# Layer 1's node work of a four-layer graph network, by quarters beside the output attention of layer 0

## The chip, the cores and the metric

The kernel runs on one core of a Trainium2 chip. The metric is the time of one execution on the device in microseconds (us), as the median of several runs. The core has a matrix engine (PE, with its weight loads as PEld), a vector engine (DVE), an activation engine (ACT), a general engine (POOL) and a queue engine (SP) that mostly issues DMAs. Each engine takes its instructions in a fixed order. "Unit", "quarter" and "count" below are words of this kernel; they are explained with it.

## The reference, cut to what matters

A graph of 4096 nodes with 64 features and a dense 0/1 adjacency passes through four layers, each of the form `x = x + layer(relu(layernorm(x)), adj)`.

```python
# layer 0: eight attention heads, then the output attention
Who = h @ W_out;  o1 = Who @ a_out[:64];  o2 = Who @ a_out[64:]
e_o = leaky_relu(o1[:, None] + o2[None, :], 0.2)
x = x + tanh(softmax(where(adj > 0, e_o, NEG)) @ Who)
# layer 1: hyperbolic attention over all pairs; h = relu(layernorm(x)), c = 1 / r**2
x_t = logmap0(h, c)                      # h * artanh(sqrt(c)*|h|) / (sqrt(c)*|h|)
left, right = x_t @ w_att[:64, 0], x_t @ w_att[64:, 0]
adj_att = sigmoid(left[:, None] + right[None, :] + b_att) * adj
support = einsum('ij,ijd->id', adj_att, logmap(h[:, None], h[None], c))
x = x + proj(expmap(h, support, c), c)
# layer 2: mean over neighbours, a dense layer, row norm
# layer 3: out[i] = sum over the last 100 neighbours j of 0.5**(later neighbours) * (h @ W3)[j]
```

In layer 1 each node needs a few numbers that come from its own row only: the squared norm `a`, `pc = 1 - c*a` and its inverse, the two scores, the scaled row, and two rows of 66 numbers ("sides") from which a single matmul gives the distances of all pairs.

## The kernel before

Nodes lie on 128 partitions in 32 blocks (`NB`); `x` and `h` are tiles of 128 x 32 x 64 floats. The adjacency comes transposed, and layer 0 leaves it in DRAM as eight-bit masks (`mask_d`) for the later layers. The program is written in one stream; a scheduler then orders each engine's instructions by its own estimates. Three helpers bind it: `in_order()` keeps the engines' instructions in the order of the program, and `behind(ins)` and `tc.issue_after(ins)` place the enclosed instructions after a given one.

**The output attention of layer 0** (the loop `for u in range(4)` and what is ahead of it). The setup takes the maxima of `who` (the 66 columns of `Who` and its two scores), reduces them over the partitions on POOL (`omax`), and makes from them the value parts `YB`, `YC`, the denominators' parts `YD1`, `YD2`, the mean `meano` and at last the negated values `YCn`. Then come four units of 1024 target nodes. A unit goes through eight mask tiles `mo` (`for q in range(NQ)`, 512 KB each, three buffers). For each, DVE makes the complement `nmo8`, which POOL's queue writes to `noedge_d` for layer 1; for every two of its four blocks ACT makes the sign of the score (`st`, L1198), DVE ands it with the mask (`B`, L1204, four buffers) and mostly makes the other edges (`C`, L1212), and PE multiplies (`acco`, L1961, and the denominators `ddo`, L1974 and L1980). At a unit's end the sums are copied to SBUF (`evD`, `evB`, `evC`); `finish_unit` transposes and divides them, takes tanh and adds to `x`. It runs inside the next unit, after its first mask tile; for the last unit it runs after the loop.

**The counts.** `count_odd` (L949, L950) loads 1 MB of the adjacency (`raw`, two buffers, SP's queue) and counts the entries that are neither 0 nor 1. There are 64 of them: 16 in the loop of the output attention (every second mask tile), 11 in layer 2, 37 in layer 3. A program with any odd entry is redone by a general kernel.

**Layer 1 before the pairs.** When all of `x` is there, `layernorm_relu()` makes `h` by halves (`norm_steps`). Then DVE computes over all 32 blocks at once: `a`, `pc`, the norm and its logarithms, `left` and `nrb` by `dot` (L2050, L2052). Five maxima (`way`) are reduced over the partitions (`wall`, L2102) to a flag `again`, which every engine reads before it branches (L2118, L2721). Behind the branch `pairs_fast` splits `left` in three parts, transposes them and sends them through DRAM to `MOV` (L2155, L2156); makes `XQ` (the rows scaled by `pabs`), and the sides `aug` for `XA` and `LD`, transposed on PE in 16 groups of four (L995) with one ACT copy each (L996). The tile `nm` of the mask work takes memory that `aug` held.

**Layer 1's pairs** (`scores`, `distances`, `factors`, `sums`) take about 545 us. `finish_steps` then gives the new `x` and `h` by quarters; `layers_fast` holds layers 2 and 3, with tiles `HH` and `SS` for the split rows of layer 2 and the values of layer 3, and `blk` for its counting matmuls. Layer 3 has four units of 1024 target nodes with eight masks `m3` of four blocks each; a count stands at the blocks that a condition on `j` and `u` picks.

Of the kernel before, what the change touches and what calls it, by code (L numbers as in the profile page):

```python
# [24 lines left out]
P = 128  # L25
# [805 lines left out]
def kernel(  # L831
# [200 lines left out]

    with ExitStack() as l0:
        lp = l0.enter_context(tc.tile_pool(name="l0", bufs=1))
        who = lp.tile([P, NB, D + 2], F32, name="who")
# [125 lines left out]
        def col_maxs(m, n, name):  # L1161

            full = lp.tile([P, n], F32, name=name)
            nc.gpsimd.partition_all_reduce(full, m, P, RMAX)
            return full
# [570 lines left out]

        HO2 = N // 4
        NK = HO2 // G
        OB = HO2 // P
        with ExitStack() as ob:  # L1740
# [21 lines left out]
            nc.gpsimd.memset(YD2, 0.0)  # L1762
            meano = hp.tile([P, NK, 2, D], F16, name="meano")
# [23 lines left out]
            with in_order():  # L1787
# [13 lines left out]
                m3 = col_maxs(m3, 4, "omax")  # L1801
                Mo = lp.tile([P, 1], F32, name="Mo")
# [68 lines left out]
            nc.vector.tensor_scalar(  # L1871
# [53 lines left out]
            for u in range(4):  # L1925
# [8 lines left out]
                for q in range(NQ):  # L1934
                    if q % 2 == 0:
                        count_odd(work, next(todo))
# [49 lines left out]
                    if q == 0 and pending:  # L1986
                        finish_unit(*pending)
                        pending = None
                evD = work.tile([P, G], F32, name="evD", tag="evD", bufs=1)
# [19 lines left out]
                pending = (u, evs)  # L2009
            finish_unit(*pending)  # L2010


    layernorm_relu()
    l1 = ctx.enter_context(ExitStack())
    lp = l1.enter_context(tc.tile_pool(name="l1", bufs=1))
    KA = D + 2

    def scalar_tile(name):
        return lp.tile([P, 1], F32, name=name)

    rt, rabs, sqc, cc = (scalar_tile(n) for n in ("rt", "rabs", "sqc", "cc"))
    nc.gpsimd.dma_start(rt, r_in.unsqueeze(0).to_broadcast([P, 1]))
    nc.vector.scalar_tensor_tensor(rabs, rt, -1.0, rt, ALU.mult, ALU.max)
    nc.vector.reciprocal(sqc, rabs)
    nc.vector.tensor_tensor(cc, rt, rt, ALU.mult)
    nc.vector.reciprocal(cc, cc)
    c2, m2c, p2c, cneg, lnr, bz, be, maxn, hrow = (
        scalar_tile(n) for n in ("c2", "m2c", "p2c", "cneg", "lnr", "bz", "be", "maxn", "hrow")
    )
    nc.vector.tensor_tensor(c2, cc, cc, ALU.mult)  # L2030
    nc.vector.tensor_scalar(m2c, cc, -2.0, None, ALU.mult)
    nc.vector.tensor_scalar(p2c, cc, 2.0, None, ALU.mult)
    nc.vector.tensor_scalar(cneg, cc, -1.0, None, ALU.mult)
    nc.vector.tensor_scalar(maxn, rabs, 1.0 - PROJ_EPS, None, ALU.mult)
    nc.vector.tensor_scalar(hrow, rabs, 0.5, None, ALU.mult)

    nc.scalar.activation(lnr, rabs, AF.Ln)
    nc.vector.tensor_scalar(bz, lnr, -1.0, -0.5 * SHIFT * LN2, ALU.mult, ALU.add)
    nc.vector.memset(be, 0.5 * SHIFT * LN2)
    wab = lp.tile([P, 2, D], F32, name="wab")  # L2040
    nc.gpsimd.dma_start(
        wab.rearrange("p s d -> p (s d)"),
        w_att.rearrange("k o -> (k o)").unsqueeze(0).to_broadcast([P, 2 * D]),
    )
    bt = scalar_tile("bt")
    nc.gpsimd.dma_start(bt, b_att.unsqueeze(0).to_broadcast([P, 1]))

    def dot(wide, pool, a, b, name):
        t = wide.tile([P, NB, D], F32, name=name + "_w", tag="wide")
        nc.vector.tensor_tensor(t, a, b, ALU.mult)  # L2050
        s = pool.tile([P, NB], F32, name=name)
        nc.vector.tensor_reduce(s, t, AX.X, ALU.add)  # L2052
        return s

    def norm_of(pool, sq, name):
        n = pool.tile([P, NB], F32, name=name)
        nc.vector.tensor_scalar(n, sq, MIN_NORM, None, ALU.max)
        nc.scalar.activation(n, n, AF.Sqrt)
        return n

    with tc.tile_pool(name="l1wide", bufs=2) as wide:
        a = dot(wide, lp, h, h, "a")
        pc = lp.tile([P, NB], F32, name="pc")
        nc.vector.tensor_scalar(pc, a, cneg, 1.0, ALU.mult, ALU.add)
        pm = lp.tile([P, NB], F32, name="pm")
        nc.vector.tensor_scalar(pm, pc, MIN_NORM, None, ALU.max)

        zn = norm_of(lp, a, "zn")
        nc.vector.tensor_scalar(zn, zn, sqc, None, ALU.mult)
        zr = small("zr")  # L2070
        nc.vector.reciprocal(zr, zn)
        nc.vector.tensor_scalar(zn, zn, CLIP, None, ALU.min)
        la, lb = small("la"), small("lb")
        nc.scalar.activation(la, zn, AF.Ln, bias=one_t, scale=1.0)
        nc.scalar.activation(lb, zn, AF.Ln, bias=one_t, scale=-1.0)
        nc.vector.tensor_tensor(la, la, lb, ALU.subtract)
        fac = lp.tile([P, NB], F32, name="fac")
        nc.vector.scalar_tensor_tensor(fac, la, 0.5, zr, ALU.mult, ALU.mult)
        left = dot(wide, lp, h, wab[:, 0:1, :].to_broadcast([P, NB, D]), "left")
        nrb = dot(wide, lp, h, wab[:, 1:2, :].to_broadcast([P, NB, D]), "nrb")  # L2080
        nc.vector.tensor_tensor(left, left, fac, ALU.mult)
        nc.vector.tensor_tensor(nrb, nrb, fac, ALU.mult)
        nc.vector.tensor_scalar(nrb, nrb, bt, -1.0, ALU.add, ALU.mult)
# [3 lines left out]
    pinv = lp.tile([P, NB], F32, name="pinv")  # L2087
    way = lp.tile([P, 5], F32, name="way")
# [12 lines left out]
    wall = lp.tile([P, 5], F32, name="wall")  # L2101
# [17 lines left out]

    def pairs_fast(es, VQ, VT, pabs):  # L2120

        fp = es.enter_context(tc.tile_pool(name="pf", bufs=1))
        XQ = VQ
        XA = fp.tile([KA, N], F32, name="XAf")
        LD = fp.tile([KA, N], F32, name="LDf")
        MOV = fp.tile([P, N], BF16, name="MOV")
# [5 lines left out]
        nc.vector.reciprocal(pinv, pc)  # L2132
        nc.vector.scalar_tensor_tensor(pabs, pinv, -1.0, pinv, ALU.mult, ALU.max)
        with ExitStack() as ss:
            wide = ss.enter_context(tc.tile_pool(name="pfwide", bufs=2))
            ps = ss.enter_context(tc.tile_pool(name="ps_pf", bufs=4, space=PSUM))

            parts = wide.tile([P, 3, NB], F32, name="parts")
            p16 = wide.tile([P, 3, NB], BF16, name="p16")
            tmp = wide.tile([P, NB], F32, name="ptmp")  # L2140
            lr_d = dram.tile([3, N], BF16, name="lr_d")
            nc.gpsimd.memset(MOV, 0.0)
            nc.gpsimd.memset(one3, 0.0)
            nc.gpsimd.memset(one3[0:3, :], 1.0)
            nc.vector.tensor_copy(tmp, left)
            for c in range(3):
                nc.vector.tensor_copy(p16[:, c], tmp)
                if c < 2:
                    nc.vector.tensor_tensor(tmp, tmp, p16[:, c], ALU.subtract)
            nc.vector.tensor_copy(parts, p16)  # L2150
# [570 lines left out]
    with tc.If(general == 0):  # L2721
        with ExitStack() as es:
# [12 lines left out]
            with ExitStack() as pe:  # L2735
                pairs_fast(pe, VQ, VT, pabs)
# [74 lines left out]
```

## Time and profile before

| what | value |
| --- | --- |
| timed runs | 2208.22, 2210.75, 2210.93 us; median 2210.75 |
| the profiled execution | 2203.01 us, span 2201.3 us, granted TensorE clock 0.93 |
| busy over the span | PE 87%, DVE 80%, ACT 73%, POOL 4% |
| output attention, setup | from about 931 us to `YCn` at 990 us |
| output attention, copies `evD` of the four units | 1034.0, 1082.4, 1128.6, 1172.9 us |
| first score matmul of layer 1 | 1236.3 us |
| last pairs, layer 2, layer 3 | to about 1780, 2028, 2195 us |

The profile is of one execution, 7.7 us under the median of the timed runs. Times in it are counted from the start of the span. In the table of windows each row gives the stretch, its length, the busy time of each engine with its number of instructions, the granted clock of PE, the mean share of the 16 DMA engines and what they moved. In a timeline each row is a start, a duration, engine, line, operation, tiles written and read, and in brackets how long the engine sat idle before it and on whom it waited. Lines are those of the kernel before unless it is said otherwise.

### The profile page before, as it was taken

Reading aid. Unit: us, or ns where it says so; the run is one execution under the profiler, and the core shown is the slowest. Engines: PE = TensorE matmul, PEld = TensorE weight load, DVE = VectorE, ACT = ScalarE, POOL = GpSimd, SP = SyncE. Lnnn points to the kernel's source line nnn. Section 1 sums busy time; section 2 is a strip of 40 time slices with the busy share of each in tenths; the row PEclk is TensorE's granted clock in tenths of the full one; section 3 lists DMA queues with packets and bytes.
Section 4 is the critical chain, followed back from the end, with each engine's and each line's share of the span. In section 5 each row is a group of like instructions: output and inputs, shape, how many; then the busy total and the mean of one; then the engine's idle time right before and its main releaser. Section 6 shows DMA issues by size and latency. Waiting matters only on the chain.

```text
span 2201.3 us, 43889 instructions
## 1 busy us (share of the span) xinstructions
PE 1916.3 (87%) x19276; PEld 865.8 (39%) x19276; DVE 1763.7 (80%) x2239; ACT 1608.9 (73%) x1379; POOL 85.5 (4%) x124
## 2 busy tenths in 40 slices
PE   4989989999999999939994679999999996889887
PEld 3444444444444444423442323333333332444222
DVE  6689989997898899978767688998989888744654
ACT  3678879997798799846773669888888873137655
POOL 1000100000000000000110000000000000000000
PEclk8999999999999999959996789999999997979989
DMA  8945554353111111078551101101110105722995
GB/s 110 185 97 93 101 84 112 126 188 121 45 45 45 45 50 50 11 259 306 177 183 43 35 15 34 34 25 29 34 35 24 34 19 199 289 104 97 315 329 216
DMA packets 117007, 239.00 MB, mean 109 GB/s; under 512 B 11059, under 2 KB 84003, under 8 KB 102051
## 3 DMA queue, kind: packets, MB, share of 16 engines
q1 hardware_dynamic: 101990, 192.92, 25.4%
q0 software_dynamic: 14816, 43.18, 11.2%
q8 instruction: 153, 2.51, 0.5%
q14 instruction: 48, 0.39, 0.1%
HBM read 245.34 MB, written 49.46 MB: 134 GB/s over the span
## 4 chain that ended last, share of the span: by engine, by line
PE 33%; DVE 16%; ACT 6%; DMA 5%; issue 4%; POOL 0%; DVEq 0%; SPq 0%; POOLq 0%; ACTq 0%
PE accj L2270 6%; PE acco L1961 4%; DMA raw<-in_adj_dram 4%; PE pu L2237 3%; PE pl L2206 2%; DVE raw L950 2%; PE pf L2308 2%; DVE at L2259 2%; PE pl L2209 2%; PE accC L1534 2%; PE nacc L2603 1%; ACT st L1198 1%; DVE at L2264 1%; PE accB L1534 1%; ACT sg L2193 1%
## 5 line engine op out<-in xcount | busy, mean ns | idle before, releaser
L1198 ACT ACTIVATE st<-srow,nt 128x2048 int8<-128x2048 f32 x352 | 682.7, 1994 | 77.2 <-DVE B L1204 76.4
L1204 DVE TENSOR_TENSOR B<-st,mres 128x1024 int32<-128x1024 int32 x256 | 311.9, 1221 | 68.1 <-PE accC L1534 44.9
L1534 PE MATMUL accB<-B,ybh 128*32 128x512 fp8e4 x3072 | 338.7, 384 | 14.4 <-DVE B L1204 14.4
L1534 PE MATMUL accD<-B,ybh 128*32 128x512 fp8e4 x2048 | 301.3, 387 | 23.6 <-DVE h L1650 23.6
L1534 PEld LDWEIGHTS <-ybh 128*32 128x32 bf16 (+1 forms) x6656 | 196.5, 98 | 238.4 <-issue 76.1
L1534 PE MATMUL accC<-mres,ych 128*32 128x512 fp8e4 x2272 | 268.1, 381 | 0.0
L1534 PE MATMUL accC<-B,ycn 128*32 128x512 fp8e4 x2272 | 267.9, 380 | 0.0
L1534 PE MATMUL accL<-B,ybh 128*32 128x512 fp8e4 x1536 | 220.0, 389 | 4.8 <-DVE h L1654 4.7
L2270 PE MATMUL accj<-sg,VQ 128*64 128x512 f32 (+1 forms) x512 | 199.5, 620 | 17.9 <-DVE sg L2311 7.0
L1534 PEld LDWEIGHTS <-ych 128*32 128x32 f16 x4096 | 168.9, 99 | 115.5 <-issue 10.2
L1192 DVE TENSOR_SCALAR st<-srow,nt 128x2048 uint8<-128x2048 f32 x160 | 205.5, 1285 | 2.5
L950 DVE SCALAR_TENSOR_TENSOR raw<-raw 128x2048 f32<-128x2048 f32 x64 | 146.3, 2288 | 65.7 <-DMA raw<-in_adj_dram 65.6
L2270 PE MATMUL acci<-sg,VQ 128*64 128x512 f32 (+1 forms) x512 | 198.9, 620 | 0.0
L2193 ACT ACTIVATE sg<-pl,rb 128x512 f32<-128x512 f32 x256 | 163.0, 684 | 48.0 <-PE pl L2209 43.7
L2689 ACT ACTIVATE w3b<-pv 128x1024 int16<-128x1024 f32 x128 | 129.6, 1023 | 73.5 <-PE pv L2680 72.4
L1198 ACT ACTIVATE st<-srowo,nto 128x1024 int8<-128x1024 f32 x128 | 137.5, 1138 | 41.7 <-DVE B L1204 41.4
L2237 PE MATMUL pu<-XAf,LDf 66*128 66x512 f32 x288 | 147.5, 615 | 8.6 <-DVE at L2244 7.4
L1534 PE MATMUL accC<-C,ych 128*32 128x512 fp8e4 x1824 | 148.0, 391 | 0.8 <-DVE C L1212 0.8
L1212 DVE TENSOR_TENSOR C<-B,mres 128x1024 int32<-128x1024 int32 x114 | 139.5, 1225 | 3.6
L1534 PEld LDWEIGHTS <-ycn 128*32 128x32 f16 x2272 | 107.5, 97 | 62.5 <-issue 1.5
L2244 DVE TENSOR_SCALAR at<-pu 128x512 f32<-128x512 f32 x144 | 95.3, 685 | 29.3 <-PE pu L2237 28.5
L2206 PE MATMUL pl<-nm,noid 128*128 128x512 fp8e4 x256 | 100.5, 393 | 10.2 <-ACT sg L2193 9.9
(499 smaller groups left out, 3099.3 us busy)
## 6 DMA issues: line engine op xcount, KB each, us to landing
raw<-in_adj_dram SPq DMA_DIRECT2D x64, 1024.0 KB, 6.0
mo<-edges SPq DMA_DIRECT2D x32, 512.0 KB, 4.6
noedge<-nmo POOLq DMA_DIRECT2D x32, 512.0 KB, 4.7
nm<-noedge SPq DMA_DIRECT2D x64, 256.0 KB, 3.0
m<-edges SPq DMA_DIRECT2D x16, 1024.0 KB, 4.8
m<-edges SPq DMA_DIRECT2D x32, 512.0 KB, 6.6
srow<-srow_d SPq DMA_DIRECT2D x15, 1024.0 KB, 6.5
mres<-in_adj_dram POOLq DMA_DIRECT2D x8, 1024.0 KB, 36.1
```

The lines of the kernel that those rows point to most:

```text
L950: nc.vector.scalar_tensor_tensor(raw, raw, 0.0, raw, ALU.is_gt, ALU.not_equal, accum_out=bad[:, c : c + 1])
L1192: nc.vector.tensor_scalar(st[:, i, :].bitcast(U8), srow, negs[:, i : i + 1], EDGE, ALU.is_gt, ALU.mult)
L1198: nc.scalar.activation(st[:, i, :], srow, AF.Sign, bias=negs[:, i : i + 1], scale=-1.0)
L1204: nc.vector.tensor_tensor(B.bitcast(I32), st.bitcast(I32), edges.bitcast(I32), ALU.bitwise_and)
L1212: nc.vector.tensor_tensor(C.bitcast(I32), B.bitcast(I32), edges.bitcast(I32), ALU.bitwise_xor)
L1534: ins = nc.tensor.matmul(acc[k * O : (k + 1) * O, :], lhsT=values, rhs=moving(k), start=start, stop=stop,)
L2193: tc.keep_in_program_order(nc.scalar.activation(*args, **kw))
L2206: nc.tensor.matmul(pl, lhsT=noid, rhs=nm[:, b, :].bitcast(F8), start=True, stop=False)
L2237: nc.tensor.matmul(pu, lhsT=LD[:, j * P : (j + 1) * P], rhs=XA[:, grp(gi)], start=True, stop=True,)
L2244: nc.vector.tensor_scalar(at[:, b, :], pu, UMIN, None, ALU.max)
L2270: nc.tensor.matmul(acc[r : r + n, :], lhsT=XQ[:, src, cols], rhs=w, start=start, stop=stop)
L2689: nc.scalar.activation(w, pv, AF.Relu)
```

## The change

1. **Layer 1's node work by quarters.** A generator `layer1_nodes` takes the norm, `a`, `pc`, `pinv`, `pabs`, the sides, both dots with their factor, and `XQ` for one quarter (eight blocks). In unit `u` of the output attention, `finish_unit` of unit `u - 1` is followed by the generator for that quarter, with one or two steps per mask tile. After the loop, `layer1_sides` transposes the sides of the three ready quarters behind the last unit's sums (`behind(sums.ins)`) and is written ahead of the last `finish_unit`; then come the last quarter's nodes and sides and `layer1_scores` (the parts of `left`, by way of DRAM to `MOV`), all ahead of the flag.
2. **Memory shared anew.** `who` gets a pool of its own, layer 0's pool is closed before the output attention, and `XQ` becomes a view of `who` (rows of 66 floats instead of 65). `XA`, `LD` and `MOV` live from the start of the output attention on; `HH` and `SS` are views of the memory of `XA`, `blk` of that of `LD`. The scalars of layer 1, their three small loads on POOL's queue and the memset of `MOV` stand ahead of the output attention. Unused scalars (`lnr`, `bz`, `be`) go.
3. **Counts held.** The 16 counts of the output attention stand behind the instruction that makes `YCn` (`behind(prepared.ins)`). In the built order DVE's counts all follow it; two of their loads are still ahead.
4. **Counts spread.** In layer 3 the condition on `j` changes: unit 0 has 12 counts instead of 10, units 1, 2 and 3 have 9, 8 and 8 instead of 9 each, at every fourth block.

```diff
+    whop = ctx.enter_context(tc.tile_pool(name="whop", bufs=1))
+    who = whop.tile([P, NB, D + 2], F32, name="who")
...
+        l0.close()
+        lq = ctx.enter_context(tc.tile_pool(name="l1", bufs=1))
...
+        XQ = who[:, :, 0:D1]
+        XA_all, LD_all = (lq.tile([P, N], F32, name=n) for n in ("XAf", "LDf"))
+        XA, LD = XA_all[0:KA], LD_all[0:KA]
+        MOV = lq.tile([P, N], BF16, name="MOV")
+        nc.gpsimd.memset(MOV, 0.0)
+
+        def layer1_nodes(bs, work, augs):
+            n = bs.stop - bs.start
+            yield from norm_steps(bs, work, "fat")
+            hb = h[:, bs]
...
+            t = fat("hh")
+            nc.scalar.activation(t, hb, AF.Square)
+            nc.vector.tensor_reduce(ab, t, AX.X, ALU.add)
+            yield False
+            nc.vector.tensor_scalar(pcb, ab, cneg, 1.0, ALU.mult, ALU.add)
...
+            nc.scalar.activation(zn, zn, AF.Sqrt)
+            nc.vector.reciprocal(pib, pcb)
...
+            nc.vector.tensor_tensor(aug[:, bs, 0:D], hb, over(pib, D), ALU.mult)
+            yield False
...
+            nc.vector.tensor_tensor(aug2[:, bs, 0:D], hb, over(cp, D), ALU.mult)
+            yield False
...
+            nc.scalar.activation(la, zn, AF.Ln, bias=one_t, scale=1.0)
+            nc.scalar.activation(lb, zn, AF.Ln, bias=one_t, scale=-1.0)
+            for i, dst in enumerate((left, nrb)):
+                t = fat("hw")
...
+                nc.vector.tensor_reduce(dst[:, bs], t, AX.X, ALU.add)
+                yield False
...
+            nc.vector.tensor_tensor(XQ[:, bs, 0:D], hb, over(pab, D), ALU.mult)
...
-            nc.vector.tensor_scalar(
+            prepared = nc.vector.tensor_scalar(
                 YCn,
...
                     if q % 2 == 0:
-                        count_odd(work, next(todo))
+                        with behind(prepared.ins):
+                            count_odd(work, next(todo))
...
                     if q == 0 and pending:
                         finish_unit(*pending)
+                        beside = layer1_nodes(slice((u - 1) * OB, u * OB), work, augs)
                         pending = None
+                    elif u:
+                        for _ in range(2):
+                            next(beside, None)
...
+            with behind(sums.ins):
+                layer1_sides(slice(0, NB - OB), ps, augs)
             finish_unit(*pending)
+            for _ in layer1_nodes(slice(NB - OB, NB), work, augs):
+                pass
+            layer1_sides(slice(NB - OB, NB), ps, augs)
+            layer1_scores(work, ps)
...
-        HH = lp.tile([P, NB, 2, D], F16, name="HH")
-        SS = lp.tile([P, NB, 2, D], F16, name="SS")
+        HH, SS = (
+            t.rearrange("p (b s d) -> p b s d", s=2, d=D)
+            for t in (XA_all.bitcast(F16)[:, 0:N], XA_all.bitcast(F16)[:, N:])
+        )
...
-            blk = lp.tile([P, NB, P], BF16, name="blk")
+            blk = LD_all.bitcast(BF16)[:, 0 : NB * P].rearrange("p (b c) -> p b c", c=P)
...
-                    if (j % 7 < 2 and j < 28 or j == 30) if u else j % 3 and j > NB // 2:
+                    if (j % 4 == 1 or j == 31 and u == 1) if u else j % 5 and j > NB // 2:
```

The built order of the changed kernel is known and is used in the prediction: on DVE units one to four of the output attention hold 8, 4, 4 and 0 counts (8, 2, 0 and 0 before, with six in the setup); on PE the 48 transposes of the first three quarters stand between the last denominators and `pdo` of the last `finish_unit`; on SP the load of `MOV` follows the reading of the flag.

## Prediction

> **What bounds the kernel now.** I read first the table of windows, cut at the marks of the output attention (the end of the setup, then each copy of the denominators, `evD`, L1990) and at the first score matmul of layer 1, to see which engine is busy where the change acts.
>
> ```profile
> core 0: us, PE busy (x) PEld busy (x) DVE busy (x) ACT busy (x) POOL busy (x), PEclk, DMA share, GB/s
> 931.00:990.30 59.30, 24.27 (x125) 14.87 (x117) 45.72 (x85) 25.94 (x40) 2.58 (x4) 0.62 0.72 248
> 990.30:1034.00 43.70, 40.22 (x252) 15.10 (x253) 38.67 (x56) 28.23 (x28) 4.29 (x6) 0.89 0.90 315
> 1034.00:1082.40 48.40, 46.04 (x319) 21.09 (x318) 34.65 (x63) 38.25 (x39) 5.87 (x9) 1.00 0.63 207
> 1082.40:1128.60 46.20, 44.99 (x314) 20.70 (x314) 31.91 (x61) 35.82 (x36) 5.74 (x9) 1.00 0.57 182
> 1128.60:1172.90 44.30, 43.53 (x308) 20.10 (x307) 25.70 (x51) 27.39 (x28) 4.75 (x7) 1.00 0.48 153
> 1172.90:1236.30 63.40, 19.26 (x111) 16.08 (x111) 46.89 (x114) 18.48 (x31) 5.98 (x7) 0.60 0.05 10
> 2028.00:2191.00 163.00, 141.47 (x628) 46.49 (x628) 91.63 (x93) 99.93 (x102) 4.92 (x7) 0.96 0.84 298
> ```
>
> Row by row: the setup is DVE's (45.7 of 59.3 us) with PE mostly idle. The first unit has DMA at 0.90 of its time and DVE at 38.7 of 43.7. Units two to four are PE's: 95 to 98% busy at full clock, with DVE free for 14 to 19 us of each. Then come 63.4 us in which PE works 19: the last unit's finish, layer 1's norm, dots and sides, one after the other on DVE. Layer 3's last 163 us run at 298 GB/s. The prize is the 63.4 us; the room for it is DVE's idle time in units two to four.
>
> Second, the timeline of DVE alone in the setup, to see what the checks of the adjacency ("counts", L950) cost there.
>
> ```profile
> 938.08 2.29 DVE L950 SCALAR_TENSOR_TENSOR raw<-raw 128x2048 f32<-128x2048 f32 x1 [0.83 <-DMA raw<-in_adj_dram]
> 940.29 0.69 DVE L1705 SCALAR_TENSOR_TENSOR x<-h,nm 128x512 f32<-128x512 f32 x1
> ...
> 955.93 2.28 DVE L950 SCALAR_TENSOR_TENSOR raw<-raw 128x2048 f32<-128x2048 f32 x1
> ...
> 967.01 2.29 DVE L950 SCALAR_TENSOR_TENSOR raw<-raw 128x2048 f32<-128x2048 f32 x1
> ...
> 976.35 2.29 DVE L950 SCALAR_TENSOR_TENSOR raw<-raw 128x2048 f32<-128x2048 f32 x1
> ...
> 983.04 2.29 DVE L950 SCALAR_TENSOR_TENSOR raw<-raw 128x2048 f32<-128x2048 f32 x1
> ```
>
> Each stands in front of a step that the setup waits for: `x` came 1.7 us late behind the first, the maxima of `who` 2.2 behind the second, the value parts 2.2 behind each of the other three.
>
> Third, the timeline of all engines between the last unit and the pairs.
>
> ```profile
> 1173.66 1.06 PE L1885 MATMUL pdo<-fold,evD 128*128 128x6 f32 x8 [0.80 <-DVE evD L1990]
> ...
> 1190.95 1.22 DVE L981 SCALAR_TENSOR_TENSOR h<-h,ln_var 128x1024 f32<-128x1024 f32 x1
> ...
> 1210.84 0.15 DVE L2117 CAST again<-wf 128x1 int32<-128x1 f32 x1
> ...
> 1211.93 3.58 DVE L2129 TENSOR_SCALAR rb<-nrb 128x32 f32<-128x32 f32 x1
> 1211.97 3.51 POOL L2142 MEMSET MOV<- 128x4096 bf16 x1 [2.64 <-DVE again L2117]
> ...
> 1223.24 9.64 PE L995 MATMUL tr<-ident,aug 128*66 128x128 f32 x64
> ...
> 1232.91 14.55 SPq L2199 DMA_DIRECT2D nm<-noedge x7
> ...
> 1236.35 0.39 PE L2206 MATMUL pl<-nm,noid 128*128 128x512 fp8e4 x1 [0.28 <-DMA nm<-noedge]
> ```
>
> The finish takes 10.5 us (1173.7 to the last `x`, 1184.1); `h` is done at 1192.2; the dots run to the flag at 1211.0; behind the branch come 25 us of memset, sides and transposes before the first score.
>
> **Setup.** Of five counts 3.9 us lie ahead of the maxima and 6.6 after. But Pool's queue now has three small loads (0.56 each at 1190.9) and the memset of `MOV` (3.5) ahead of the all-reduce of the maxima, and the loads wait for the last reads of layer 0's memory: after the last `pwho` (about 954) that is 954 + 1.7 + 3.5 = 959.2, then 0.4, so the maxima are back at about 960 against 961.6. The `rb` row (32 columns, 3.58 us beside the memset, where its like take 0.2) says that DVE's `tensor_scalar`s may stand still meanwhile. I take 1.5 + 6.6 = 8 us saved, bounds 4 and 10. Two complements `nmo` (0.6 each) come in and as many mask products move out: nothing.
>
> **First unit.** It keeps eight counts; DVE's queue sums to 40.7 us against 38.9 (masks 0.60 us apart, counts 2.29). DMA was at 0.90, the held counts' transfers still share SP's queue with the masks, and a count's load waits for DVE to free one of two buffers, with the next mask behind it. I take +1; bounds -3 and +6.
>
> **Units two to four.** A quarter of layer 1 (1,024 rows) puts on DVE seven operations and five reductions of 128x512 at 0.6 and some twenty small ones at 0.1 to 0.15: 10 us. Units two and three also take four counts each, where they had two and none. My sum over the built order gives 45.6 us for two and for three, 33.4 for four; the same sum gave 33.2, 29.3 and 23.7 before. At the first unit's rate of filling (38.7 of 43.7, or 0.885) two and three need 51.5 each, against 48.4 and 46.2: +3 and +5. Four needs 37.7 of 44.3: 0. At full filling it would be 0 in all; at the 0.77 of the setup row 59 each, +24. I take +8, bounds 0 and +24. ACT's part of a quarter is 2.2 us of short activations and up to three table loads.
>
> ```profile
> 1182.81 1.28 ACT L978 ACT_TABLE_LOAD   x1
> 1184.11 0.31 ACT L978 ACTIVATE ln_var<-ln_var,consts 128x16 f32<-128x16 f32 x1
> ```
>
> The next activation starts 1.30 us after the load, so a quarter costs ACT 2.2 + 3 x 1.3 = 6.1 us and unit three has 35.8 + 6.1 = 41.9 of 46.2: covered, though with 4 us left. The Trainium skill ("ScalarE: Activation LUTs", What ACT_TABLE_LOAD costs) speaks against this change: it adds a drain of about 1.38 us, 2.66 in all per switch. By that rule, as an estimate, unit three would hold 46 us of ACT and each unit would lose another 2 or so; the rows show no drain, and the sum goes by them.
>
> **The end of the last unit.** PE's new order puts 48 transposes of the three ready quarters in front of `pdo`, so they delay the finish. 64 took 9.64 us with four PSUM buffers (a group of four 0.60, its ACT copy 0.58); with two buffers and ACT handing back each, 12 groups at about 0.7 are 8.3 us (7.2 without any wait, 14 if copies and transposes alternate). So `pdo` comes at +8.7 after `evD` (+0.8 before), and `x` 10.5 later, at +19.2. The last quarter's norm is 5 us (the second half's took 8.0 from 1184.2 to `h`, 1.2 of it the first half's last step; half of the rest and a table load); from `h` to the flag eight 128x512 steps (4.8), the 5.5 us of small steps that lay there before, and some 2 of sides and parts: 12. Then 0.9 for the branch and 3.4 from the issue of `nm` to the first score (1232.91 to 1236.35), with `MOV`'s load landing before that: +41.4 in all, against 63.4. That is -22, bounds -16 and -26. What is gone behind the branch is the memset, three sweeps of 2.2 us, 16 transposed groups and the wait of `nm` for the memory of `aug`.
>
> **The pairs and layer 2** keep their order but for the first matmuls; `XQ` in `who` has rows of 66 instead of 65 floats, and the shared `XAf`/`LDf` memory brings no new wait in layer 2's order: 0, bounds ±2.
>
> **Layer 3.** The 37 counts stay, so do their bytes. SP's order has pairs of counts ahead of a mask 13 times instead of 12, then single ones. A pair with its mask took 8.0 us (issues at 2036.9 to 2125.3, eleven steps), PE needs 5.2 for one mask's four blocks (four by 1.30). Before, pairs stand also in the last unit, which ran 2144.7 to 2190.6, 46 us for 41.6 of work; after, its eight masks go at PE's pace. -3, bounds -6 and +2.
>
> **Sum.** -8 + 1 + 8 - 22 - 3 = -24. The profiled run was 2203.0 (span 2201.3 and 1.7 around it), the median of the three timed runs 2210.75, 7.7 above it; the same 24 us off gives 2179 there and 2186.8 here: 2187.
>
> **The rivals.** (1) *The room is not there.* DVE's queue is in order, and the layer-1 steps raise its filling to the setup's 0.77, +24 instead of +8; the flag then comes 16 us later: 2203. For it: units two and three would be 99% full at PE's pace; against: four mask buffers of slack. (2) *Slower: DVE waits on ACT.* Each quarter has five places where DVE needs an ACT result (two squares, two roots, the logarithms) queued behind signs of 1.06 us, which wait in turn for DVE's masks. If each costs five signs, the most that stand between two of these steps in ACT's built order, 15 x 5.3 = 80 us are lost, less the 14 us by which the three sums (45.6, 45.6, 33.4) stay under the windows: +66 in place of +8, so 2187 + 58 = 2245. It decides from 3.3 us a wait on (8 + 28 + 14 = 50 us over 15). Against it: DVE waited for ACT's signs only 1.8 us between 1020 and 1180. (3) *The holding does nothing for the setup* (Pool's queue and the memset eat it, the first unit stays DMA-bound) and the transposes alternate with their copies: +8 and +6, 2201.
>
> **How the numbers follow.** Forecast as summed, within its terms' bounds: 0.66, its own range 2178 to 2197. Rival 1: 0.12; rival 3: 0.11; rival 2: 0.06; a better case, units at full filling and -26 at the end (2175): 0.05. About 0.2% (4.4 us) is what a measurement of this kernel can tell from no change, so faster means below 2206.3. Rival 1's upper tail gives 0.05 of same, rival 3's 0.01; slower is rival 2 and a little of 1. The range 2174 to 2204 leaves out rival 2, the tails of 1 and 3 and half the better case.
>
> **What would show it.** In the profile after: `YCn` about 8 us earlier with no count ahead of it; `evD` copies 50 us apart for units two and three with DVE above 0.85 there; the last `evD` near 1174; `pdo` 8 to 9 us after it; the first score 41 us after it with PE's first distance matmul waiting for nothing of ACT; layer 3's last unit at 42 to 43 us. Wrong it is if `evD` copies stand over 58 us apart, or if the first score is over 50 us behind the last `evD`.

## The result, and the profile after

The changed kernel takes 2192.85 us (median of 8 runs, 2188.22 to 2199.66), the kernel before 2206.82 us (8 runs, 2201.60 to 2210.93). The ratio is 0.994 with a 95% interval of 0.9923 to 0.9957: faster by about 13 us, where 24 were forecast. The time lies 6 us above the predicted 2187 and inside the range 2174 to 2204.

The table of windows of the changed kernel, cut at its own marks: `YCn`, the four copies `evD`, the first score matmul; the last row is layer 3.

```profile
core 0: us, PE busy (x) PEld busy (x) DVE busy (x) ACT busy (x) POOL busy (x), PEclk, DMA share, GB/s
931.00:980.50 49.50, 19.78 (x82) 13.36 (x80) 34.06 (x80) 22.85 (x37) 8.89 (x10) 0.61 0.53 171
980.50:1025.60 45.10, 40.47 (x260) 15.38 (x260) 39.96 (x57) 31.33 (x31) 4.28 (x6) 0.94 0.87 320
1025.60:1077.50 51.90, 46.66 (x313) 21.05 (x313) 46.07 (x99) 40.19 (x45) 5.71 (x8) 0.97 0.76 253
1077.50:1129.70 52.20, 47.21 (x312) 21.11 (x311) 46.76 (x99) 40.97 (x45) 5.70 (x8) 0.93 0.59 208
1129.70:1174.60 44.90, 44.90 (x315) 20.64 (x314) 34.98 (x84) 35.61 (x40) 4.99 (x7) 1.00 0.47 153
1174.60:1211.40 36.80, 19.88 (x112) 12.96 (x112) 22.62 (x98) 16.00 (x28) 0.81 (x3) 0.72 0.05 13
2008.30:2181.50 173.20, 150.31 (x628) 47.41 (x628) 91.77 (x92) 100.19 (x101) 4.93 (x7) 0.89 0.80 281
```

The setup is 10 us shorter; units two and three are longer, and DVE's work in them (46.1 of 51.9 us, 46.8 of 52.2) has come up to PE's (46.7 and 47.2); the stretch to the first score fell from 63.4 to 36.8 us; layer 3 moved 281 GB/s instead of 298 and took longer. Its four unit ends in the timeline of DVE, the copies of the sums:

```profile
2012.92 0.69 DVE L2724 COPY ev<-sacc 128x512 f32<-128x512 f32 x1
...
2065.82 0.69 DVE L2724 COPY ev<-sacc 128x512 f32<-128x512 f32 x1 [0.44 <-PE sacc L2679]
...
2137.82 0.69 DVE L2724 COPY ev<-sacc 128x512 f32<-128x512 f32 x1 [2.15 <-PE sacc L2679]
...
2181.80 0.69 DVE L2724 COPY ev<-sacc 128x512 f32<-128x512 f32 x1 [5.85 <-PE sacc L2679]
```

They stand 52.9, 72.0 and 44.0 us apart; in the first profile of the kernel before it was 49.0, 63.1 and 46.6. The pairs began 25 us earlier, but the end came only 9 us earlier. So the study asks where 16 us went behind the first score of the pairs (5 of them ahead of layer 3, 10 in it), and which parts of the change earned what came before it. Each kernel was profiled a second time (e1 and e9 below), because the stages of one execution vary; the two columns of each kernel show by how much.

| stage, us | before (two profiles) | changed (two profiles) | forecast | measured |
| --- | --- | --- | --- | --- |
| to `YCn` | 989.9, 991.4 | 980.1, 979.6 | -8 | -10.8 |
| `YCn` to the last `evD` | 183.0, 182.6 | 194.5, 193.0 | +9 | +11.0 |
| last `evD` to the first score | 63.4, 63.0 | 36.8, 37.8 | -22 | -25.9 |
| first score to the first copy `VT` of the pairs | 44.0, 44.1 | 46.2, 49.8 | 0 | +4.0 |
| from there to the first `ev` of layer 3 | 752.3, 753.0 | 755.3, 752.0 | 0 | +1.0 |
| three units of layer 3 (first to last `ev`) | 158.6, 165.1 | 168.9, 162.3 | -3 | +3.8 |
| last `ev` to the end of the span | 10.0, 10.7 | 10.8, 10.8 | 0 | +0.5 |
| sum | | | -24 | -16.6 |

### The profile page after: what moved, and what is told of

Same layout as the page of the kernel before. It is cut to its first block, busy times and chain, and to the rows that moved or that the text cites. A ratio compares the mean times of both kernels' runs of the same rounds, so it can differ in the third digit from the quotient of the medians.

```text
span 2192.6 us, 43992 instructions
## 1 busy us (share of the span) xinstructions
PE 1923.9 (88%) x19276; PEld 865.5 (39%) x19276; DVE 1765.8 (81%) x2330; ACT 1623.2 (74%) x1402; POOL 84.7 (4%) x124
## 4 chain that ended last, share of the span: by engine, by line
PE 30%; DVE 14%; issue 12%; ACT 6%; DMA 2%; POOL 0%; POOLq 0%; SPq 0%; DVEq 0%; ACTq 0%
PE accj L2292 6%; PE pu L2259 3%; PE acco L2097 3%; PE pl L2228 2%; PE pf L2330 2%; PE pl L2231 2%; DVE at L2281 2%; PE accC L1536 2%; DMA mo<-edges 2%; PE nacc L2628 1%; ACT sg L2215 1%; PE accB L1536 1%; ACT xt L2215 1%; DVE at L2286 1%; ACT root L2215 1%
## 5 line engine op out<-in xcount | busy, mean ns | idle before, releaser
L2292 PE MATMUL accj<-sg,who 128*64 128x512 f32 (+1 forms) x512 | 199.6, 619 | 17.8 <-DVE sg L2333 6.9
L2292 PE MATMUL acci<-sg,who 128*64 128x512 f32 (+1 forms) x512 | 199.1, 618 | 0.0
L2266 DVE TENSOR_SCALAR at<-pu 128x512 f32<-128x512 f32 x144 | 95.3, 684 | 20.0 <-PE pu L2259 19.2
L2228 PE MATMUL pl<-nm,noid 128*128 128x512 fp8e4 x256 | 99.8, 390 | 10.5 <-ACT sg L2215 8.9
## 6 DMA issues: line engine op xcount, KB each, us to landing
mres<-in_adj_dram POOLq DMA_DIRECT2D x8, 1024.0 KB, 35.9
```

Of the source, the lines that this page charges most:

```text
L2228: nc.tensor.matmul(pl, lhsT=noid, rhs=nm[:, b, :].bitcast(F8), start=True, stop=False)
L2266: nc.vector.tensor_scalar(at[:, b, :], pu, UMIN, None, ALU.max)
L2292: nc.tensor.matmul(acc[r : r + n, :], lhsT=XQ[:, src, cols], rhs=w, start=start, stop=stop)
```

## The experiments

Ratios are to runs of the kernel before on the same chip (e1 to e4 share one, e5 to e8 another, e9 to e12 a third), with 95% intervals. 0.0001 is 0.22 us.

**e1, the changed kernel again.**

> The changed kernel once more, for the rate of layer 3's transfers. In the first profile the copies of layer 3's sums stood 52.9, 72.0 and 44.0 us apart, with 297 and 306 GB/s in units two and three; in the kernel before 49.0, 63.1 and 46.6 us, with 321 and 325 GB/s. The bytes of the three units together were the same (48.3 and 48.4 MB). Theory A (the spread of the counts costs it): the same distances again, 52 to 54 and 71 to 73 us, and 300 to 308 GB/s. Theory B (the rate is that of one execution, not of the kernel): the rate is another, say 315 GB/s and more, and units two and three together take 113 to 119 us instead of 124.9.

Ratio 0.9933 (0.9913 to 0.9953). Units two to four of layer 3 took 48.7, 69.6 and 44.0 us at 323, 323 and 231 GB/s. Theory B's numbers were met: the rate was another one (323 instead of 297 and 306), and units two and three took 118.3 us. Yet unit three still took 69.6, more than the 63.1 at 325 GB/s in the first profile of the kernel before. With the new spread 16 counts run in unit three, with the old one 15, since the counts of unit one are let go late and worked off in the units behind it.

**e2, the old spread of layer 3's counts in the changed kernel.**

```diff
-                    if (j % 4 == 1 or j == 31 and u == 1) if u else j % 5 and j > NB // 2:
+                    if (j % 7 < 2 and j < 28 or j == 30) if u else j % 3 and j > NB // 2:
```

> The changed kernel with the old condition for the counts of layer 3 (same 37 counts, 10 and 9 a unit, instead of 12, 9, 8, 8). Theory A: units two and three together go back to about 112 to 115 us, the last to 46.6, and the time is 8 to 10 us under that of the changed kernel beside it. Theory B: at the same rate as the changed kernel beside it units two and three take 5 us less (1.5 MB less at 306 GB/s) and the last one 2.6 more, so the time is 2 us less or the same.

Ratio 0.9937 (0.9920 to 0.9955), against 0.9933 for e1: no difference. The units took 52.0, 63.5 and 46.1 us at 303, 321 and 266 GB/s, 161.6 in all against e1's 162.3. The 8 to 10 us of theory A are excluded.

**e10, the new spread alone, in the kernel before**, the same line the other way round.

> The kernel before with one part of the change alone: the new condition for layer 3's counts (12, 9, 8, 8 a unit instead of 10, 9, 9, 9). The last unit then has 8 single counts and goes at TensorE's pace (44.0 us instead of 46.6), and units two and three take one or two counts more. My prediction: 3 us less in all. What the profiles with this condition point to (162.3 to 168.9 us for units two to four, against 158.6 to 163.1 with the old one): 2 to 6 us more, all of it in unit three (68 to 70 us instead of 63.5).

Ratio 0.9991 (0.9976 to 1.0007): -2 us with 3 on either side; the units took 50.3, 70.7 and 44.0. So the last unit gains 2.6 us and unit three is as long as in e1, yet no loss shows in the time. The forecast of -3 stands inside this interval, but a zero does too; the 2 to 6 us more that the profiles pointed to lie outside it.

**e9, the kernel before again.**

> The kernel before once more, for the stages behind the first score, which no edit of its order changes. In its first profile 796.3 us lay between the first score and the first copy of layer 3's sums, and 158.6 us between that copy and the last; the kernel with only the counts held, whose code there is the same, had 800.3 and 163.1. If that is the rate of one execution: another profile of the kernel before gives 798 to 802 and 160 to 164 us, with 300 to 318 GB/s in units two and three. If the earlier start of the pairs costs something of itself: 795 to 797 and 158 to 160 us again.

Ratio 0.9996 (0.9980 to 1.0012), as it must be. It settled half of the question: 49.1, 69.2 and 46.8 us at 318, 299 and 258 GB/s. The kernel before, with its old spread, has units that sum to 158.6 us in one execution and 165.1 in another. But 797.1 us lay between the first score and the first copy of layer 3, near the 796.3 of its other profile, and 801.5 and 801.8 in the changed kernel. The table above shows where that half sits: at the very start of the pairs. (e5, in the old order, has 800.3 us as well, but its extra 4 us lie behind the first `VT`, which came after 44.0.)

The windows around that start, first of e9, then of e1: the 5.29 us ahead of the first score (in e1 all the time since the flag was computed), then twice 10 us:

```profile
1231.78:1237.07 5.29, 4.10 (x26) 2.66 (x24) 0.69 (x1) 3.29 (x7) 0.00 (x0) 1.00 0.31 91
1237.07:1247.07 10.00, 9.19 (x33) 3.97 (x33) 5.61 (x7) 7.61 (x11) 0.00 (x0) 1.00 0.39 109
1247.07:1257.07 10.00, 9.06 (x24) 3.17 (x22) 7.79 (x9) 9.55 (x7) 0.00 (x0) 1.00 0.09 26
```

```profile
1205.17:1210.46 5.29, 3.77 (x4) 1.20 (x5) 2.97 (x15) 0.00 (x0) 0.43 (x2) 0.50 0.35 104
1210.46:1220.46 10.00, 9.99 (x17) 3.94 (x18) 4.42 (x5) 4.33 (x6) 0.00 (x0) 0.50 0.21 61
1220.46:1230.46 10.00, 10.00 (x32) 3.98 (x30) 6.04 (x7) 7.20 (x10) 0.00 (x0) 0.95 0.24 71
```

The column behind POOL is the granted clock of PE. In these rows of the kernel before it is 1.00; in the changed kernel it is 0.50 in the first 16 us, and from the first score on PE gets through 17 matmuls in 10 us where it had 33, though it is busy all the time. Before, the transposes of the sides ran behind the branch, right ahead of the first pairs, and the clock rose among them (at 1228.3 in the first profile, 5 us behind the first transpose); now PE is idle for most of the 18 us before the flag (its last finish matmul ends at 1187.7, the flag comes at 1205.8 in the first profile). In every profile of a kernel with the new order the first `VT` came 46.2 to 50.2 us after the first score, in the four with the old order after 44.0 or 44.1. The ten also say how much of this is the clock. Behind the first score it stood at 0.50 for another 3.4 us (first profile of the changed kernel) to 11.8 us (e12), with PE busy throughout. Half of that stretch is the delay against 44.0 within 0.5 us in each of the ten: 1.7 against 2.1 in the changed kernel, 5.5 against 5.8 in e1, 5.9 against 6.2 in e12. So the clock accounts for the 4 us. The remedy is not tested: no run kept PE busy in that gap on purpose.

**e3, the ready quarters' sides behind the last finish.**

```diff
+                    yield
...
-            with behind(sums.ins):
-                layer1_sides(slice(0, NB - OB), ps, augs)
             finish_unit(*pending)
-            for _ in layer1_nodes(slice(NB - OB, NB), work, augs):
+            ready = layer1_sides(slice(0, NB - OB), ps, augs)
+            steps = layer1_nodes(slice(NB - OB, NB), work, augs)
+            for _ in steps:
+                for _ in range(2):
+                    next(ready, None)
...
```

> The changed kernel with the transposes of the three ready quarters behind the last finish on TensorE, and their copies between the steps of the last quarter's norm on ScalarE, instead of ahead of pdo. In the changed kernel pdo stood 8.3 us after evD behind 48 transposes, and the first score 36.8 us after it. If the path from evD to the first score is the finish, the norm and the flag on VectorE: pdo about 1.5 us after evD, the first score 30 to 32 us after it, and the time 5 us less. If ScalarE's copies (two in 1.30 us) only come to stand in front of the norm's square instead: first score 35 to 37 us after evD, the time the same within 2 us.

The `yield` stands in `layer1_sides`, after each group of four transposes. Ratio 0.9917 (0.9899 to 0.9935), e1 beside it 0.9933: not told apart. `pdo` stood 0.7 us after `evD` (1.5 expected), 7.6 us earlier than in the changed kernel, but the first score came 35.9 us after `evD`, a gain of 1 to 2 us only, as the second forecast had it. The clock again, first in the changed kernel (the transposes, then the finish), then in e3 (the finish in three pieces):

```profile
1174.50:1183.00 8.50, 7.28 (x55) 4.59 (x51) 1.81 (x3) 6.58 (x13) 0.00 (x0) 1.00 0.00 0
1183.00:1188.00 5.00, 4.69 (x40) 4.55 (x40) 2.61 (x12) 1.66 (x2) 0.00 (x0) 1.00 0.00 0
```

```profile
1181.00:1184.00 3.00, 2.62 (x18) 2.04 (x18) 1.59 (x7) 0.49 (x1) 0.00 (x0) 1.00 0.00 0
1184.00:1185.50 1.50, 1.41 (x12) 1.35 (x11) 1.11 (x5) 0.10 (x1) 0.00 (x0) 0.88 0.00 0
1185.50:1188.50 3.00, 3.00 (x16) 3.00 (x16) 0.89 (x4) 0.00 (x0) 0.00 (x0) 0.50 0.00 0
```

In the rows of the changed kernel PE keeps 1.00 through the whole finish, which takes 6.8 us (1182.9 to the last `x` at 1189.7). In e3 the clock is halved in the midst of it and the finish takes 11.3 us (1181.4 to 1192.7). But the clock is only a part of this, as two other profiles show, e1 with the transposes ahead and e5 without them:

```profile
1181.00:1183.90 2.90, 2.90 (x26) 2.90 (x26) 1.23 (x7) 1.70 (x2) 0.00 (x0) 1.00 0.00 0
1183.90:1187.30 3.40, 3.34 (x17) 3.15 (x16) 1.12 (x5) 0.00 (x0) 0.00 (x0) 0.50 0.00 0
```

```profile
1165.70:1171.40 5.70, 5.54 (x42) 4.77 (x42) 3.24 (x14) 0.86 (x2) 0.00 (x0) 1.00 0.00 0
```

In e1 the clock fell in the midst of the finish too, and it took 8.3 us; in e5 the clock held through PE's part of it, and it took 8.6. Of the eight profiles with the transposes ahead, four have a finish of 6.8 us (clock held) and four of 7.9 to 8.3 (clock fell about 3 us behind the start of `pdo`). The three of the old order whose clock fell have 10.1 to 10.9. So the clock is worth 1 to 2 us of the finish, and the order about 2: without the transposes the last matmuls of `acco` and the copies `evC` come in between the finish's steps, as does a step of the first half's norm in the old order; with them the sums are copied meanwhile.

Against the changed kernel's first profile e3 has `pdo` 7.6 us earlier, the finish 4.5 longer (2 of it a table load of ACT that came to stand behind a copy of the sides), the norm 1.7 longer behind other such copies, and 0.4 more in the rest. That makes the gain of 1.

**e5, only the counts held, in the kernel before**, and **e6, the changed kernel without the holding**:

```diff
-                        count_odd(work, next(todo))
+                        with behind(prepared.ins):
+                            count_odd(work, next(todo))
```

> The kernel before with one part of the change alone: the output attention's counts held until YCn. Theory (the counts stood ahead of the setup's steps on VectorE): YCn 6 to 8 us earlier, near 982 to 984, the first evD 6 to 8 us earlier too, and the whole time 6 to 8 us less; the changed kernel's setup had 9.8 us less (989.9 to 980.1), of which the rest would be the smaller maxima path. Rival (the first unit's transfers take it back, its DMA share is 0.90): YCn earlier by as much, but the first unit 4 to 8 us longer than 43.7 us, and the time the same within 2 us.

> The changed kernel without the holding of the counts. Theory: YCn 6.6 to 10 us later (near 987 to 990), units two and three shorter by up to 4 us together, since one or two counts fewer stand in each, and the time 4 to 8 us above that of the changed kernel. Rival (the setup's gain is given back by units two and three, which the held counts fill to 0.89 on VectorE): the last evD comes at the same time within 2 us, and so does the end.

e5: ratio 0.9979 (0.9963 to 0.9995), about 5 us faster, where 6 to 8 were expected; `YCn` at 978.9, the last `evD` at 1164.9, 8 to 9 us earlier than in the two profiles of the kernel before. Alone, the holding pays, and the first unit takes back only part (45.8 us). e6: ratio 0.9909 (0.9884 to 0.9934), not slower than the changed kernel's 0.9933 but equal or a little better; `YCn` at 986.8 and the last `evD` at 1173.9, inside the 1172.6 to 1174.6 of the changed kernel. So here the rival is right: beside the node steps the holding is worth nothing. The windows of units two and three say why, e6 first, then e7, which holds the counts and has no node steps there:

```profile
1034.24:1082.10 47.86, 44.32 (x304) 20.20 (x304) 44.24 (x98) 38.57 (x44) 5.70 (x8) 0.96 0.73 258
1082.10:1129.21 47.11, 45.60 (x317) 20.95 (x316) 40.42 (x93) 41.51 (x47) 5.69 (x8) 1.00 0.54 179
```

```profile
1026.54:1077.68 51.14, 47.09 (x317) 21.37 (x317) 45.26 (x71) 36.83 (x38) 5.70 (x8) 0.98 0.89 309
1077.68:1123.03 45.35, 44.69 (x312) 20.48 (x311) 30.41 (x60) 35.88 (x37) 5.91 (x9) 0.99 0.54 180
```

Node steps without held counts leave unit three at 47.1 us (46.2 before); held counts without node steps leave it at 45.4; both together make it 52.2 and 50.7, with 46.8 us of DVE's work in it. Unit two pays some 3 us for the held counts alone (51.1, DMA at 0.89) and nothing for the nodes alone. Each part by itself fits under PE's pace in unit three; the two do not fit together.

**e7, the node steps of all four quarters behind the last `evD`.**

```diff
-                        beside = layer1_nodes(slice((u - 1) * OB, u * OB), work, augs)
                         pending = None
-                    elif u:
-                        for _ in range(2):
-                            next(beside, None)
...
-                nc.vector.tensor_copy(evD, dd)
+                denoms = nc.vector.tensor_copy(evD, dd)
...
-            with behind(sums.ins):
-                layer1_sides(slice(0, NB - OB), ps, augs)
             finish_unit(*pending)
...
+            for u in range(4):
+                bs = slice(u * OB, (u + 1) * OB)
+                with behind(denoms.ins):
+                    for _ in layer1_nodes(bs, work, augs):
+                        pass
+                    layer1_sides(bs, ps, augs)
```

> The changed kernel with the main part undone: the steps of layer 1 for all four quarters, and their sides, come behind the last evD, none beside the output attention; the counts stay held and spread. Theory (VectorE's room in units two to four is what pays): units two and three 47 to 49 us instead of 51.9 and 52.2, the last evD 6 to 8 us earlier, but the first score 65 to 72 us behind it instead of 36.8, three quarters of 10 us more on VectorE and the slow finish of the kernel before; the time 20 to 28 us above that of the changed kernel. Rival (what pays is the work taken out of the path, the old memset, sweeps and loads, not the place of the steps): first score 50 us behind evD, and the time within 8 us of the changed kernel's.

Ratio 1.0042 (1.0021 to 1.0063), 24 us above the changed kernel's 0.9933: slower than the kernel before. The last `evD` came at 1167.4 (7 us earlier) and the first score 65.1 us behind it, of which DVE worked 51.3 (22.6 of 36.8 in the changed kernel). The rival, that removing the old memset and sweeps is what pays, would have had 50 us there; it falls. What pays is the place of the steps.

**e4 and e8, layer 3's counts let go earlier**, four and two groups of layer 2 before its last; **e11 and e12**, the same two without the holding.

```diff
-                        with tc.issue_after(valued[-1].ins):
+                        with tc.issue_after(valued[-4].ins):     # e8 and e12: valued[-3]
```

> The changed kernel with layer 3's counts let go four groups of layer 2 earlier (behind the fourth-last group's values, not the last's). In the changed kernel the first unit of layer 3 ran beside layer 2's last groups with a DMA share of 0.24 and no count in it, and units two and three were at 0.85 and 0.89 (52.9 and 72.0 us), the last at TensorE's pace (44.0). If the transfers of the counts bound units two and three: some 13 counts of 1 MB move into the idle 48 us, units two and three come near 44 to 50 us each, and the time falls by 15 to 30 us. If VectorE's 2.3 us of each count lengthen layer 2's chain of norms instead (13 x 2.3 = 30 us at most): the first unit's end comes 15 to 30 us later and the time stays within 5 us.

> The changed kernel with layer 3's counts let go two groups of layer 2 earlier than the changed kernel does, where four groups earlier brought units two to four of layer 3 to 46.3, 48.6 and 46.0 us but made the second late come 81 to 88 us after the first instead of 66.5. If each count ahead of that late costs it 1.6 us (21 us for 13 counts): with some 10 counts ahead it comes 8 to 16 us later than in the changed kernel instead of 21, units two to four stay at 46 to 52 us, and the time is 3 to 8 us under that of the kernel with four groups earlier. If the transfers bound it all the same (37 counts in less time), units two and three lengthen by as much, and the time is the same within 3 us.

> The changed kernel without the holding of the counts, and with layer 3's counts let go four groups of layer 2 earlier: the two edits that each were below the changed kernel. If they add up (the one acts before the pairs, the other behind them): 0.991 times 0.9945 = 0.9855 of the kernel before, near 2175 us, with the last evD near 1173 and units two to four of layer 3 at 46 to 49 us. If the not-holding is worth nothing by itself, 0.988, near 2181 us.

> The same without the holding, with layer 3's counts let go two groups earlier instead of four: 10 counts ahead of the second late instead of 13. Four groups earlier gave 0.9879 and two 0.9918, on different chips, while the profiles had two groups ahead (958.5 us from the first score to the last copy, against 960.2). If those profiles decide, this is 1 to 3 us below the kernel with four groups on the same chip; if the ratios do, 6 to 8 us above it.

| kernel | ratio | second `late` after the first | units two to four of layer 3 |
| --- | --- | --- | --- |
| e1, changed kernel | 0.9933 (0.9913 to 0.9953) | 66.9 | 48.7, 69.6, 44.0 |
| e4, four groups | 0.9879 (0.9862 to 0.9896) | 88.3 | 46.3, 48.5, 46.0 |
| e8, two groups | 0.9918 (0.9896 to 0.9940) | 85.5 | 47.3, 47.6, 45.0 |
| e11, four groups, not held | 0.9876 (0.9849 to 0.9902) | 86.7 | 44.4, 48.5, 45.9 |
| e12, two groups, not held | 0.9879 (0.9857 to 0.9902) | 87.4 | 50.9, 47.0, 43.5 |

Both forecast mechanisms act at once. The stretch of layer 2's last groups beside layer 3's first unit, in the changed kernel and in e4:

```profile
1960.00:2007.57 47.57, 47.21 (x258) 21.81 (x257) 15.79 (x47) 35.55 (x54) 0.40 (x1) 1.00 0.24 75
```

```profile
1960.00:2029.16 69.16, 53.65 (x259) 25.62 (x257) 49.47 (x78) 35.55 (x54) 1.57 (x1) 0.84 0.76 266
```

The idle DMAs (0.24) are put to use (0.76) and units two to four take 141 us in all instead of 162 to 169, but the counts stand in DVE's queue ahead of layer 2's norms and that stretch grows by 21 us. 12 us remain by the ratios of e4 and e1, somewhat under the 15 expected. The expectations counted wrongly what stands ahead of the second `late`: the traces have 15 counts there with four groups (e4, e11) and 11 with two (e8, e12). Either number costs 19 to 21 us, so a count costs 1.3 to 1.9 us and not a fixed 1.6; letting go two groups earlier instead of four saves nothing there, and e8 missed its forecast of 8 to 16 us.

Letting the holding go as well adds nothing that can be measured with four groups (0.9876 against 0.9879), but the interval of e11 also holds the 0.9855 that was expected if it did. With two groups 0.9879 stands against 0.9918 (e12 and e8, on different chips, with intervals that just overlap). On one chip e11 and e12 are equal within 7 us, which decides neither forecast of e12. So what the holding is worth beside the earlier counts stays open. e4, e11 and e12 are the best versions, about 27 us under the kernel before and 12 to 13 under the changed kernel.

## Why the prediction was right, and where it was off

- **Setup, -8.** Right in the main: -10.8. No count stands ahead of `YCn`, as foretold. The stall of DVE beside the memset that I allowed for came: a `tensor_scalar` of 128 x 2 took 2.41 us (see the last section). What I mis-sized is when POOL's loads start: at 951.8 us and not behind 954, so the maxima were back at 957.6 and not at 960.
- **First unit, +1, and units two to four, +8.** Right in sum (+11.0) and nearly in place: 45.1 (from the end of `YCn`), 51.9, 52.2 and 44.9 us against 44.7, 51.5, 51.5 and 44.3. The filling of 0.885 taken from the first unit was the right row: 0.89 and 0.90. Rival 1's 0.77 falls, and rival 2 with it: it needed 50 us of waits, and the units are 11 longer in all.
- **The price of a table load.** ACT had 41.0 us of work in unit three, against 41.9 by the rows and an estimated 46 by the Trainium skill ("ScalarE: Activation LUTs", What ACT_TABLE_LOAD costs). In the last norm a load started at 1192.06 and the root behind it at 1193.35, 1.29 us later. No drain of 1.38 us shows, and the sum was right to go by the row.
- **The end of the last unit, -22.** Measured -25.9. `pdo` came at +8.3 us (8.7 forecast), the last norm took 4.9 (5) and the path from `h` to the flag 11.2 (12). The step that was off is the finish, taken at 10.5 us from the kernel before; it took 6.8 and, in e1, 8.3. With the transposes in front the last sums are copied out meanwhile, and in half of the profiles the clock holds to its end. From the flag to the first score it was 5.6 us (4.3 forecast). The prediction's sum for this path also does not come out of its terms: 19.2 + 5 + 12 + 0.9 + 3.4 is 40.5 and not 41.4, so by its own terms it was -23.
- **The pairs, 0.** Off by +4.0, outside the bounds of 2: the same transposes had brought the clock up for the first pairs. I had costed them as 9.6 us of work to be moved and never as what the clock goes by.
- **Layer 3, -3.** The profiles say +3.8, but two of one kernel differ by 7; the runs of the spread alone say -2 with 3 on either side, which contains the forecast. The last unit at 42 to 43 us was near (44.0). What I left out is that one more count then goes through unit three, whose DMAs are the busiest (0.89 in it, 0.92 before): 306 GB/s over 72.0 us are 22.0 MB, where 325 over 63.1 were 20.5. It took 69 to 72 us with the new spread in all six profiles that have it, 63 to 69 in the four with the old one. The rest of the first profile's 10 us goes with the lower rate of that execution.
- **Sum.** -24 was forecast, -13 measured by the ratio, -16.6 by the table. About 4 us of the gap are the start of the pairs. Layer 3 is up to 7 by the profiles, at most 4 or 5 by the runs of the spread alone. The other rows miss by 1 to 4 us each and partly cancel. That 2187 lies only 6 us off is partly luck: it counts from 2210.75, the median of three runs of the kernel before, and the median of eight is 2206.82; the same 24 us off that would be 2183.
- **Rival 3** (0.11) had one outcome right: beside the node steps the holding gains nothing, and without it (e6) the last `evD` comes at the same time. Its reason was wrong. The setup did gain, the first unit was not longer for it, and units two and three gave it back, which the forecast had as two separate terms.

## What to carry to other kernels

Work that fills an idle engine beside a bound one can be worth most of its length (e7 against the changed kernel: 29 us of DVE's work left the path, and the time fell by 24), but two such fillings into the same gap are not the sum of both: each of the held counts and the node steps fitted under PE's pace in unit three, and together they filled DVE as far as PE and made the unit 4 to 6 us longer. Ask of every block of matmuls that is moved what clock it was holding up, at the place it leaves as well as where it goes. And before a term of 3 us is argued over in a stage bound by transfers, profile the same kernel twice: that stage alone moved by 7 us between executions.

## What the runs showed of the hardware

- **PE's granted clock falls although PE is busy.** In e3 it went from 1.00 to 0.50 about 5 us after the last dense matmul, with mostly f32 matmuls of 64 or 6 columns filling 87 to 100% of the time, where 128-column f32 transposes at 86% held it at 1.00 for 8.5 us in the changed kernel. It fell 3.8 to 8.7 us behind the last dense matmul in the six profiles without transposes there, and 11.3 to 16.8 us behind it in the eight with them.
- **It can come back late.** The Trainium skill ("TensorE: Matmul & The Clock Gate", Part 1: The HAM clock gate) states that about 3.4 us of sustained work bring the full clock back. These rows run from the first score to the full clock, in the changed kernel's first profile and in e1:

```profile
1211.38:1214.80 3.42, 3.42 (x7) 1.47 (x8) 0.00 (x0) 2.25 (x3) 0.00 (x0) 0.50 0.66 195
1210.46:1221.50 11.04, 11.04 (x19) 4.09 (x20) 4.42 (x5) 4.61 (x6) 0.00 (x0) 0.50 0.25 72
```

The first is as the page says, the second is not: PE was busy for 11.0 us and had half the clock. In the other eight profiles of the new order it took 8.6 to 11.8 us, and the measurement decides. What makes the difference stays open.

- **The rate of transfers is that of an execution.** Unit two of layer 3, with the same instructions, moved 297, 323, 304 and 301 GB/s in four kernels that do not differ there (the changed kernel, e1, e3, e6), and took 48.7 to 52.9 us. What sets it stays open.
- **DVE stood still beside POOL's memset.** The timeline of the changed kernel's setup:

```profile
953.36 3.54 POOL L1777 MEMSET MOV<- 128x4096 bf16 x1
...
954.51 2.41 DVE L1932 TENSOR_SCALAR mx<-mx 128x2 f32<-128x2 f32 x1
956.96 0.17 DVE L1935 TENSOR_TENSOR m<-mx 128x4 f32<-128x4 f32 x1
```

Two columns took 2.41 us and ended with the memset at 956.9; the operation after it took 0.17. In e5, which has no memset there, the same `tensor_scalar` took 0.17 us. It stands on the way to the maxima, so by these rows, as an estimate, a memset placed elsewhere would save some 2 us. That was not tried.
